# GpSimd's small operations in the order of the text, other places for loads, and a product of seven for the first key projection

## The chip, the cores and the metric

The kernel runs on one core of a Trainium2 chip. The metric is the device time of one execution in microseconds (us). One profiled execution gives the trace; its engines are called PE (TensorE: matmuls), DVE (VectorE), ACT (ScalarE), POOL (GpSimd) and SP (which only issues transfers). ACT and POOL issue transfers too. "PEclk" is the share of full speed that TensorE's clock was granted.

## The reference

Four images of 512 channels and 32x32 positions go through four layers. Each layer normalizes its input over groups of 16 channels and adds its result to the input.

```python
x = x + _L0_conv_ref(_gn(x), ...)   # attention, heads mixed, softmax, attention normalized
x = x + _L1_conv_ref(_gn(x), ...)   # a gate for each channel
x = x + _L2_conv_ref(_gn(x), ...)   # plain attention
x = x + _L3_conv_ref(_gn(x), mempool, 8)  # top 8 of 2048 memory rows
```

- Layer 0 projects queries, keys and values (512x512 weights), forms the scores of 8 heads over 1024x1024 positions, mixes the heads by an 8x8 matrix, takes the softmax, normalizes every head's map by its mean and variance, multiplies by the values and projects.
- Layer 1 takes the mean of every channel, runs 512 amplitudes through a small simulated circuit of 9 qubits (rotations and sign products), and turns 9 results by one more matrix and a sigmoid into a factor for each channel.
- Layer 2 is attention with 8 heads without mixing. Layer 3 looks up memory rows.

All data are 32-bit floats.

## The kernel before

**Stages.** The program first loads image 0, normalizes it, makes its queries (`first`), makes constants (`circuit`) and image 0's keys (`take_k`, line 457). Then layer 0 runs for image 0 to 3 (265 to 290 us each), with the gate of layer 1 of the image before tucked in. Layers 2 and 3 follow. From layer 2 on a flag, `by_scalar`, is set.

**A step of layer 0** (`step`) handles 32 query positions of all heads; an image has 32 steps and 7 more that drain the pipeline ("the tail"). In step s, PE forms scores in two halves (line 510), ACT copies each to the tile `ss` (line 516), and eight transfers, the relays, rearrange the two halves into `s2` (shown as `s<-ss`, line 525): four issued by SP, four by POOL. `ss` has two buffers. Two steps later PE mixes heads (line 536), ACT takes exponentials (line 543), and DVE transposes (549) and gathers statistics (564). From step 7 on PE multiplies by the values (575). Sums of rows (`sums`), their inverses and the scaling of outputs on POOL (`scale`, line 648) go on every four steps.

**Work of other images inside the steps.** `state["plan"]` is a table from step to loads, called by `early` between the two halves of the scores. It holds `next_image` (the next image's rows into `xn_all` in 256 KB halves, and four column blocks of its query weights), and for images 1 to 3 `collect` (the attention output of the image before back into `xn_all`, and its projection weights). These loads are issued by ACT (`beside`). From step OUT = 12 on, `put_quarter` projects a quarter of a block of the previous image's output in each step, in the bank `pt`, and adds it on DVE (727) to `xr`, a piece of the input that `image_piece` loads at the end of the odd step before.

**Chains in moves.** `mid` advances several generators by one move in each step: the normalization of the next image (`prepare`, at steps 9 to 12 and later), the normalization of the attention maps (`instance_norm`, steps 3 to 6), and `state["behind"]`, the gate of the image before (`gating`). A chain alternates tiny matmuls in `pt` (lines 152, 162, 929, 934, 944, 959), copies by DVE, and tiny POOL operations (157 to 159, 126, 909, 922 to 926, 939, 955 and others).

**What sets the order.** Each engine runs its instructions in one order. An instruction wrapped in `pin` keeps the place that it has in the text; the others are placed by a scheduler that works with priorities and estimated times. Nearly all of PE, DVE and ACT in layer 0 is pinned; of POOL the relays and `sums` are, the chains' small operations are not.

**Products of seven.** `seven` multiplies 2x2 blocks with seven products instead of eight, from sums of blocks that DVE makes (`sums_k`, `add7` and `sub7`, all recorded as line 1041). It serves the key projection of images 1 to 3 (`seven_keys`, matmuls in line 1112) and most projections of layer 2, at the border between two images. There `behind` moves once after each product, as the gate does in `seven_keys`.

Of the kernel before, what the change touches and what calls it, by code (L numbers as in the profile page):

```python
# [41 lines left out]
def fast_net(ctx: ExitStack, tc: tile.TileContext, a: dict, out: bass.AP, flag: bass.AP):  # L42
# [88 lines left out]

    def take_small(dst, ps):

        if by_scalar:
            nc.scalar.copy(dst, ps)
        else:
            pin(nc.vector.tensor_copy(dst, ps))


    def group_coeffs_parts(mean, var, tag):  # L140
# [4 lines left out]
        hold = pin if n == 1 else lambda ins: ins  # L145
# [11 lines left out]
        hold(nc.gpsimd.tensor_sub(dm, mean, gm))  # L157
        hold(nc.gpsimd.tensor_mul(sq, dm, dm))
        hold(nc.gpsimd.tensor_add(sq, sq, var))
# [11 lines left out]
        hold(rsqrt(rstd, ve))  # L171
# [98 lines left out]
    def next_image(b, key, src):  # L270
# [8 lines left out]
        halves = [half(k, n) for k in range(KC) for n in range(T // NB)]  # L279
        plan = {NEXT - 8 + 2 * i: halves[i:i + 1] for i in range(4)}  # L280
# [142 lines left out]
    def prepare(b):  # L423
# [5 lines left out]
        nc.gpsimd.tensor_mul(ybar, dm, rstd)  # L429
        nb = small.tile([P, KC], F32, tag="nb", name=f"nb{b}")  # L430
        nc.gpsimd.tensor_mul(nb, gm, rstd)
        nc.gpsimd.tensor_scalar_mul(nb, nb, -1.0)
# [222 lines left out]
    def collect(b):  # L655
# [10 lines left out]
        def w(m):  # L666
# [4 lines left out]
            OUT - 2: [part(1, 1)], OUT - 1: [w(0)], OUT: [w(1)], OUT + 1: [part(2, 0)],  # L671
            OUT + 2: [w(2)], OUT + 3: [part(2, 1)], OUT + 4: [w(3)], OUT + 5: [part(3, 0)],
            OUT + 6: [part(3, 1)],
# [9 lines left out]
    def instance_norm(b):  # L683
# [7 lines left out]
        nc.gpsimd.tensor_scalar(by_head, of_head, red, None, ALU.mult)  # L691
# [7 lines left out]
        nc.gpsimd.tensor_scalar_add(al, al, IN_EPS)  # L699
        rsqrt(al, al)  # L700
        nc.gpsimd.tensor_mul(al, al, gamma)
        bb = small.tile([P, NH], F32, tag="ibb", name=f"ibb_{b}")
        nc.gpsimd.tensor_scalar_mul(bb, al, -1.0 / T)
        nc.gpsimd.tensor_add(bb, bb, beta)
        nc.gpsimd.tensor_mul(bb, bb, I["vsum"])
# [49 lines left out]
    def put_quarter(b, i):  # L755
# [3 lines left out]
        m, n4 = unit(i)[0], 2 * unit(i)[1] + i % 2  # L759
        Q = NB // 2  # L760
        ps = small_ps(f"p_{b}_{i}")[:, 0:Q]
        o = out_view(b)
        for k in range(KC):
            pin(nc.tensor.matmul(  # L764
                ps, I["w_p"][:, k, m * P:(m + 1) * P], o[:, n4, k],
                start=(k == 0), stop=(k == KC - 1),
            ))
        add_to(b, m, I["xr", m, n4 // 2][:, n4 % 2 * Q:(n4 % 2 + 1) * Q], ps)
        if n4 % 2:
            piece_done(b, m, n4 // 2)  # L770
# [44 lines left out]
    def circuit():  # L815
# [11 lines left out]
        pin(nc.vector.tensor_scalar_mul(m, m, SCALE))  # L827
        pin(nc.vector.tensor_mul(
# [25 lines left out]
        nc.scalar.activation(sincos, ang, AF.Sin)  # L854
# [1803 lines left out]
```

## Time and profile before

| | before |
| --- | --- |
| device time, median of 3 runs | 2538.16 us (2535.89 to 2540.12) |
| the profiled execution's own time | 2539.05 us |
| its span | 2537.3 us |
| PE busy | 2482.0 us, 98% |
| DVE busy | 1803.6 us, 71% |
| POOL busy | 1217.8 us, 48% |
| ACT busy | 1019.2 us, 40% |
| granted PE clock, mean | 0.996 |
| moved by transfers | 367.19 MB, 145 GB/s |

A row of the timeline has the start, the duration, the engine, the line and the operation with what it writes and reads; "x4" counts merged instructions, and the bracket is the idle time of the engine just before, with what ended it. A matmul of 128x512 in 32-bit floats shows as two records. An engine with "q" behind its name is its queue of transfers. In a list of waits the last three numbers are the total, how many times, and the longest. The rows of windows give for every engine the busy time and, in brackets, its instructions, then PEclk, the mean busy share of the 16 transfer engines, and what they moved per second.

### The profile page before, as it was taken

To read this page: it belongs to the slowest core of one execution; us is meant where nothing else is said; L and a number is where in the kernel's file an instruction comes from. 1 tells how busy PE (TensorE), PEld (TensorE's weight loads), DVE (VectorE), ACT (ScalarE), POOL (GpSimd) and SP (SyncE) were. 2 spreads that over 40 slices of the span, in tenths; PEclk is the share of its full clock that TensorE was granted. 3 is DMA by queue.
4 is the path that set the end of the run, shared out by engine and by line. 5 is a ranking of instruction groups with operands and counts; after the bars stand their busy time and mean duration, and the time that the engine had idled before them with its cause. 6 is when DMAs were issued, how large, how long until landed. Compare 5 with 4: busy or idle time off the path is not lost.

```text
span 2537.3 us, 48070 instructions
## 1 busy us (share of the span) xinstructions
PE 2482.0 (98%) x18520; PEld 1177.2 (46%) x18520; DVE 1803.6 (71%) x2940; ACT 1019.2 (40%) x1237; POOL 1217.8 (48%) x1688
## 2 busy tenths in 40 slices
PE   9999999999999999999999999999999999999998
PEld 4344534554355534545633633453363344444445
DVE  4599568875688548885768777576857648787876
ACT  1467346651665336651254145225314612121211
POOL 2266425553355525553185147117405616666665
PEclk9999999999999999999999999999999999999999
DMA  2578548872698528893211330131114046767666
GB/s 84 146 205 236 132 126 222 240 219 73 175 238 235 145 73 210 241 246 136 76 47 54 116 128 18 63 104 51 44 44 150 18 141 180 222 182 222 181 189 176
DMA packets 190031, 367.19 MB, mean 145 GB/s; under 512 B 32985, under 2 KB 96473, under 8 KB 185570
## 3 DMA queue, kind: packets, MB, share of 16 engines
q1 hardware_dynamic: 109712, 186.58, 23.7%
q0 software_dynamic: 49152, 142.79, 20.6%
q10 hardware_dynamic: 30930, 34.66, 5.1%
q8 instruction: 149, 2.44, 0.4%
q14 instruction: 88, 0.72, 0.1%
HBM read 190.10 MB, written 39.58 MB: 91 GB/s over the span
## 4 chain that ended last, share of the span: by engine, by line
PE 65%; issue 10%; POOL 10%; DVE 7%; DMA 5%; ACT 2%; SPq 0%; POOLq 0%; ACTq 0%; DVEq 0%
PE pair L1112 11%; PE pair L1358 7%; PE pv L575 7%; PE pair L199 7%; POOL got L1535 7%; PE pair L510 6%; PE pair L536 5%; PE pt L468 5%; PE pair L1238 4%; PE pt L1395 4%; PE pt L764 3%; PE pv L1395 3%; DMA s<-ss 2%; ACT e L543 2%; DVE eT L1377 1%
## 5 line engine op out<-in xcount | busy, mean ns | idle before, releaser
L549 DVE STREAM_TRANSPOSE eT<-e 128x1024 f32<-128x1024 f32 x256 | 316.6, 1237 | 203.3 <-ACT e L543 202.7
L525 POOL DMA_DIRECT2D s<-ss x512 | 258.0, 511 | 393.9 <-PE pair L536 128.5
L1535 POOL DMA_INDIRECT got<-in_mem,ix x256 | 279.7, 1093 | 214.2 <-DVE tmx L1541 142.0
L1352 ACT ACTIVATE eT<-pair 128x1024 f32<-128x1024 f32 x256 | 248.2, 1022 | 319.9 <-PE pair L1358 158.0
L564 DVE BATCH_NORM_STATS2 st<-e 128x6 f32<-128x256 f32 x1024 | 350.7, 404 | 0.0
L1376 POOL TENSOR_TENSOR e<-eT 128x1024 f32<-128x1024 f32 x96 | 240.4, 2507 | 166.8 <-ACT eT L1352 122.3
L543 ACT ACTIVATE e<-pair 128x1024 f32<-128x1024 f32 x256 | 250.5, 1022 | 164.3 <-PE pair L536 134.2
L516 ACT COPY ss<-pair 128x1024 f32<-128x1024 f32 x256 | 247.3, 1019 | 86.1 <-DMA s<-ss 44.0
L510 PE MATMUL pair<-k,q 64*32 64x512 f32 x4096 | 268.1, 600 | 12.8 <-ACT e L543 12.8
L575 PE MATMUL pv<-eT,v 128*64 128x128 f32 x4096 | 250.7, 276 | 4.0 <-ACT pv L635 4.0
L575 PEld LDWEIGHTS pv<-eT,v 128*64 128x64 f32 x4096 | 221.1, 137 | 71.7 <-issue 55.2
L1358 PE MATMUL pair<-q,k 64*128 64x512 f32 x1024 | 240.0, 605 | 2.0 <-DVE sum L1041 0.9
L1377 DVE TENSOR_TENSOR eT<-eT,e 128x1024 f32<-128x1024 f32 x96 | 142.5, 1485 | 129.4 <-POOL e L1376 129.2
L1372 POOL TENSOR_TENSOR eT<-eT 128x1024 f32<-128x1024 f32 x32 | 83.4, 2606 | 201.3 <-ACT eT L1352 197.4
L536 PE MATMUL pair<-s,wmix 32*32 32x512 f32 x4096 | 160.9, 602 | 6.9 <-DMA s<-ss 5.4
L1582 DVE SCALAR_TENSOR_TENSOR acc<-got,et,acc 128x512 f32<-128x512 f32 x210 | 157.9, 752 | 7.5
L1358 PEld LDWEIGHTS pair<-q,k 64*128 64x128 f32 x1024 | 92.2, 186 | 140.4 <-issue 66.4
L1515 ACT COPY att<-pair 128x1024 f32<-128x1024 f32 (+1 forms) x65 | 64.9, 999 | 221.2 <-PE pair L1510 212.4
L510 PEld LDWEIGHTS pair<-k,q 64*32 64x32 f32 x4096 | 57.2, 105 | 181.0 <-ACT e L543 86.9
L1041 DVE TENSOR_TENSOR k<-k,pair 128x512 f32<-128x512 f32 (+1 forms) x80 | 67.9, 893 | 78.3 <-PE pair L1112 62.1
L1530 DVE MAX8 top<-att 128x8 f32<-128x2048 f32 x31 | 71.1, 2293 | 73.0 <-issue 40.8
L1510 PE MATMUL pair<-memT,xn_d 128*128 128x512 f32 x256 | 120.7, 594 | 0.0
(380 smaller groups left out, 3737.5 us busy)
## 6 DMA issues: line engine op xcount, KB each, us to landing
s<-ss SPq DMA_DIRECT2D x512, 128.0 KB
s<-ss POOLq DMA_DIRECT2D x512, 128.0 KB
rb<-r POOLq DMA_DIRECT2D x64, 128.0 KB
o<-o SPq DMA_DIRECT2D x32, 256.0 KB
xr_c<-x SPq DMA_DIRECT2D x32, 256.0 KB
rb_c<-r SPq DMA_DIRECT2D x64, 128.0 KB
eT<-x SPq DMA_DIRECT2D x32, 256.0 KB
out<-eT SPq DMA_DIRECT2D x32, 256.0 KB
```

The costliest lines, as they stand in the source:

```text
L510: pin(nc.tensor.matmul(sc[m * NS:(m + 1) * NS, r, :], q[r * HD:(r + 1) * HD, m, s * NS:(s + 1) * NS], k_[r * HD:(r + 1) * HD, m, n * NB:(n ...
L516: pin(nc.scalar.copy(ss[:, :, n * NB:(n + 1) * NB], sc))
L525: pin(relays[side].dma_start(out=s2[2 * m + r::NH], in_=ss[m * NS:(m + 1) * NS, r, :]))
L536: pin(nc.tensor.matmul(mixed(s, r // 2)[t * NS:(t + 1) * NS, r % 2, :].rearrange("p (qq k) -> p qq k", qq=2), wmix[r * NS:(r + 1) * NS], s ...
L543: pin(nc.scalar.activation(e[:, half].rearrange("p r qq k -> p (r qq k)"), flat2(mixed(s, half)), AF.Exp))
L549: pin(nc.vector.transpose(eT[:, j % 2].rearrange("p b (qq i r) x -> p i r qq b x", qq=2, i=4)[:, i, 2 * half:2 * half + 2], e[:, half].rea ...
L564: pin(nc.vector.bn_stats(st[:, i, 2 * half + r, qq, :], e[:, half, r, qq, :]))
L575: pin(nc.tensor.matmul(pv[r * HD:(r + 1) * HD, gp, :], I["v"][:, t, g * HD:(g + 1) * HD], eT[:, j % 2, t, :, 4 * g:4 * g + 4], start=(t == ...
L1112: pin(nc.tensor.matmul(ps[:, m, :], w[:, k, m * P:(m + 1) * P], x[:, k, :], start=(k == 0), stop=(k == 1)))
L1352: pin(nc.scalar.activation(e, scs[len(es)], AF.Exp, scale=SCALE))
L1358: pin(nc.tensor.matmul(sc[:, r, :], I["k"][r * HD:(r + 1) * HD, m, t * P:(t + 1) * P], I["q"][r * HD:(r + 1) * HD, m, n * NB:(n + 1) * NB] ...
L1535: pin(nc.gpsimd.indirect_dma_start(out=got[:, i, :], out_offset=None, in_=a["mem"], in_offset=bass.IndirectOffsetOnAxis(ap=ix[:, i:i + 1], ...
```

## The change

- `kept` pins POOL's small operations of the chains as long as `by_scalar` is not set, so in the whole of layer 0; before only calls with one column were pinned.
- For image 1 alone, `next_image` puts its eight half rows and four weight columns one to a step at steps 8 to 19 (before: steps 20 to 33). `collect` swaps some outputs and weight columns between steps 12 and 18.
- `image_piece` is issued in the even step, by `early`, behind the step's other loads. `put_half` writes alternate halves of the bank.
- The first keys come from `seven_keys(0)`; `circuit` becomes a generator whose rotations go between the products.
- In `seven` a function `between` is called after the matmuls of each product and ahead of their evacuation. The gate moves there (`go_on`), leaves the last three steps of the tail, and has one move more before its second rotation. In image 3's tail it goes on into `seven_v`.
- At layer 2's border `behind` moves after products 3, 4, 6 and 7 of the first seven, not after each. The sums of Wq for image 1 start two units earlier.

```diff
     by_scalar = []
 
+    def kept(ins):
+        return ins if by_scalar else pin(ins)
+
...
         n = mean.shape[1]
-        hold = pin if n == 1 else lambda ins: ins
...
         dm, sq = tile_("dm"), tile_("gsq")
-        hold(nc.gpsimd.tensor_sub(dm, mean, gm))
-        hold(nc.gpsimd.tensor_mul(sq, dm, dm))
-        hold(nc.gpsimd.tensor_add(sq, sq, var))
+        kept(nc.gpsimd.tensor_sub(dm, mean, gm))
+        kept(nc.gpsimd.tensor_mul(sq, dm, dm))
+        kept(nc.gpsimd.tensor_add(sq, sq, var))
...
         yield
         rstd = tile_("grstd")
-        hold(rsqrt(rstd, ve))
+        kept(rsqrt(rstd, ve))
...
         halves = [half(k, n) for k in range(KC) for n in range(T // NB)]
+        if b == 1:
+            columns = [load_columns(b, key, a[key], m) for m in range(KC)]
+            return {TC + i: [load] for i, load in enumerate(halves + columns)}
         plan = {NEXT - 8 + 2 * i: halves[i:i + 1] for i in range(4)}
         plan |= {NEXT + i: halves[4 + 2 * i:6 + 2 * i] for i in range(2)}
         plan |= {NEXT + 2 + m: [load_columns(b, key, a[key], m)] for m in range(KC)}
...
-        nc.gpsimd.tensor_mul(ybar, dm, rstd)
+        kept(nc.gpsimd.tensor_mul(ybar, dm, rstd))
         nb = small.tile([P, KC], F32, tag="nb", name=f"nb{b}")
-        nc.gpsimd.tensor_mul(nb, gm, rstd)
-        nc.gpsimd.tensor_scalar_mul(nb, nb, -1.0)
+        kept(nc.gpsimd.tensor_mul(nb, gm, rstd))
...
             OUT - 5: [part(0, 0)], OUT - 4: [part(0, 1)], OUT - 3: [part(1, 0)],
-            OUT - 2: [part(1, 1)], OUT - 1: [w(0)], OUT: [w(1)], OUT + 1: [part(2, 0)],
-            OUT + 2: [w(2)], OUT + 3: [part(2, 1)], OUT + 4: [w(3)], OUT + 5: [part(3, 0)],
-            OUT + 6: [part(3, 1)],
+            OUT - 2: [part(1, 1)], OUT - 1: [w(0)], OUT: [part(2, 0)], OUT + 1: [w(1)],
+            OUT + 2: [part(2, 1)], OUT + 3: [w(2)], OUT + 4: [part(3, 0)],
+            OUT + 5: [w(3), part(3, 1)],
...
-        nc.gpsimd.tensor_scalar(by_head, of_head, red, None, ALU.mult)
+        kept(nc.gpsimd.tensor_scalar(by_head, of_head, red, None, ALU.mult))
...
-        nc.gpsimd.tensor_scalar_add(al, al, IN_EPS)
-        rsqrt(al, al)
-        nc.gpsimd.tensor_mul(al, al, gamma)
+        kept(nc.gpsimd.tensor_scalar_add(al, al, IN_EPS))
+        kept(rsqrt(al, al))
+        kept(nc.gpsimd.tensor_mul(al, al, gamma))
...
-    def put_quarter(b, i):
...
+    def put_half(b, i):
...
+        (m, n), half = unit(i), i % 2
...
-        ps = small_ps(f"p_{b}_{i}")[:, 0:Q]
+        ps = small_ps(f"p_{b}_{i}")
...
         for k in range(KC):
             pin(nc.tensor.matmul(
-                ps, I["w_p"][:, k, m * P:(m + 1) * P], o[:, n4, k],
-                start=(k == 0), stop=(k == KC - 1),
+                ps[:, half * Q:(half + 1) * Q], I["w_p"][:, k, m * P:(m + 1) * P],
+                o[:, 2 * n + half, k], start=(k == 0), stop=(k == KC - 1),
             ))
-        add_to(b, m, I["xr", m, n4 // 2][:, n4 % 2 * Q:(n4 % 2 + 1) * Q], ps)
-        if n4 % 2:
-            piece_done(b, m, n4 // 2)
+        add_to(b, m, I["xr", m, n][:, half * Q:(half + 1) * Q], ps[:, half * Q:(half + 1) * Q])
+        if half:
...
         pin(nc.vector.tensor_scalar_mul(m, m, SCALE))
+        yield
         pin(nc.vector.tensor_mul(
...
         pin(nc.vector.tensor_scalar(ang, ang, lim, -lim, ALU.min, ALU.max))
-        nc.scalar.activation(sincos, ang, AF.Sin)
+        yield
+        pin(nc.scalar.activation(sincos, ang, AF.Sin))
+        yield
...
-        for i in range(NP):
-            for l, m in ((0, turn[:, 0:1]), (1, turn[:, 1:3])):
-                rotate(
...
+        for i in range(NP):
+            for l, m in ((0, turn[:, 0:1]), (1, turn[:, 1:3])):
+                rotate(
...
+                )
+                yield
...
-        nc.gpsimd.tensor_mul(y, dm, rstd)
+        kept(nc.gpsimd.tensor_mul(y, dm, rstd))
...
-                    nc.gpsimd.tensor_scalar_mul(us[:, n], u, a_)
+                    kept(nc.gpsimd.tensor_scalar_mul(us[:, n], u, a_))
...
-                nc.gpsimd.tensor_sub(u_v[:, :, 0], cos_v[:, :, 0], sin_v[:, :, 1])
-                nc.gpsimd.tensor_add(u_v[:, :, 1], cos_v[:, :, 1], sin_v[:, :, 0])
+                kept(nc.gpsimd.tensor_sub(u_v[:, :, 0], cos_v[:, :, 0], sin_v[:, :, 1]))
+                kept(nc.gpsimd.tensor_add(u_v[:, :, 1], cos_v[:, :, 1], sin_v[:, :, 0]))
             return u
 
         u = yield from turned(0, lambda ps: pin(nc.tensor.matmul(
             ps[:, 0:KC], turn[:, 0], y, start=True, stop=True)))
         yield
+        if not by_scalar:
+            yield
...
-        nc.gpsimd.tensor_mul(pr, u, u)
+        kept(nc.gpsimd.tensor_mul(pr, u, u))
...
-        nc.gpsimd.tensor_mul(zr[:, 0:1], zr[:, 0:1], zr[:, 1:2])
+        kept(nc.gpsimd.tensor_mul(zr[:, 0:1], zr[:, 0:1], zr[:, 1:2]))
...
-        nc.gpsimd.tensor_add(gate, gate, fcb)
+        kept(nc.gpsimd.tensor_add(gate, gate, fcb))
...
-        nc.gpsimd.tensor_mul(s1, rstd, gate)
-        nc.gpsimd.tensor_mul(t1, gm, s1)
-        nc.gpsimd.tensor_scalar_mul(t1, t1, -1.0)
-        nc.gpsimd.tensor_scalar_add(s1, s1, 1.0)
+        kept(nc.gpsimd.tensor_mul(s1, rstd, gate))
+        kept(nc.gpsimd.tensor_mul(t1, gm, s1))
+        kept(nc.gpsimd.tensor_scalar_mul(t1, t1, -1.0))
+        kept(nc.gpsimd.tensor_scalar_add(s1, s1, 1.0))
...
-        nc.gpsimd.tensor_mul(sa, s1, rstd)
-        nc.gpsimd.tensor_sub(ta, t1, gm)
-        nc.gpsimd.tensor_mul(ta, ta, rstd)
+        kept(nc.gpsimd.tensor_mul(sa, s1, rstd))
+        kept(nc.gpsimd.tensor_sub(ta, t1, gm))
+        kept(nc.gpsimd.tensor_mul(ta, ta, rstd))
         tb = I["tb"] = small.tile([P, KC], F32, tag="tb", name=f"tb_{b}")
-        nc.gpsimd.tensor_add(tb, t1, bp2)
+        kept(nc.gpsimd.tensor_add(tb, t1, bp2))
...
         for i, (at, uses) in enumerate(SEVEN):
             ps = next_pair()
             multiply(ps, *factors[at])
+            if between:
+                between()
             for *ij, op in uses:
                 if put:
...
-    def seven_keys(b):
...
-    def seven_by_channels(b, name, bias):
...
-                     lambda i, j: dst[:, 2 * i:2 * i + 2, j * NB:(j + 1) * NB], begin)
-
-    def seven_v(b):
+                     lambda i, j: dst[:, 2 * i:2 * i + 2, j * NB:(j + 1) * NB], begin,
+                     between=between)
+
+    def seven_v(b, between=None):
...
     first()
-    circuit()
-    for m in range(KC):
-        take_k(0, m, m + 1)
+    constants = circuit()
+    next(constants)
+    key_sums = sums_k(0)
+    run_some(key_sums, 4)
+    next(constants)
+    for i, _ in enumerate(seven_keys(0)):
+        next(key_sums, None)
+        next(constants)
+    run_out(constants)
...
-        if b > 0 and OUT <= s + 1 < OUT + 16 and s % 2:
-            image_piece(b - 1, *unit(s + 1 - OUT))
         if not putting:
             mid(b, s)
...
+    def go_on():
+        next(state["behind"], None)
+
     def early(b, s):
 
         for load in state["plan"].get(s, ()):
             load()
+        if b > 0 and OUT <= s < OUT + 16 and s % 2 == 0:
+            image_piece(b - 1, *unit(s - OUT))
 
...
         elif b > 0 and OUT <= s < OUT + 16:
-            put_quarter(b - 1, s - OUT)
+            put_half(b - 1, s - OUT)
...
         for s in range(STEPS, STEPS + LAG):
-            step(b, s, lambda b, s: next(state["behind"], None),
+            step(b, s, lambda b, s: go_on() if s < STEPS + KC else None,
                  lambda b, s: qs[s - STEPS](s + 1) if s < STEPS + KC else None)
...
-            for i, _ in enumerate(seven_by_channels(0, "k", bk2)):
-                next(state["behind"], None)
+            for i, _ in enumerate(seven_by_channels(0, "k", bk2, go_on)):
...
-        for m, _ in enumerate(() if last else seven_keys(b + 1)):
-            next(state["behind"], None)
+        for m, _ in enumerate(() if last else seven_keys(b + 1, go_on)):
...
-            for i, _ in enumerate(seven_v(0)):
+            for i, _ in enumerate(seven_v(0, go_on)):
...
-            if s == 9 and b == 0:
+            if s == 7 and b == 0:
                 weights = weight_sums(1, "Wq")
-            if s >= 10 and b == 0:
+            if s >= 8 and b == 0:
                 next(weights, None)
...
-            next(behind, None)
+            if i in (2, 3, 5, 6):
+                next(behind, None)
...
```

## The prediction

> **What bounds the kernel now.** I read the head of the page first, then the list of waits of TensorE, then the timeline around each of its longest waits.
>
> ```profile
> span 2537.3 us, 48070 instructions
> ...
> PE 2482.0 (98%) x18520; PEld 1177.2 (46%) x18520; DVE 1803.6 (71%) x2940; ACT 1019.2 (40%) x1237; POOL 1217.8 (48%) x1688
> ```
>
> TensorE is busy for all but 55 us, so the change can win in two ways: fewer matmuls, or fewer of TensorE's waits. These waits bear on the change (total us, times, longest):
>
> ```profile
> PE pair L536 <- DMA s<-ss: 5.4, 4, 2.4
> PE pt L934 <- POOL amp L926: 5.4, 3, 2.5
> PE pt L152 <- DVE eT L1452: 5.0, 2, 2.6
> ...
> PE pt L944 <- POOL pr L939: 1.9, 2, 1.0
> ...
> PE pt L929 <- DVE ri L602: 1.4, 1, 1.4
> ```
>
> They make 19 us. Some cost more than the list says, since the granted clock falls after them. Windows of 10 us around three of them (the number after the POOL column is the clock):
>
> ```profile
> 256.00:266.00 10.00, 8.30 (x128) 2.98 (x128) 5.72 (x13) 7.29 (x8) 5.64 (x14) 0.83 1.04 235
> 594.00:604.00 10.00, 8.55 (x25) 3.83 (x22) 1.56 (x3) 2.64 (x5) 8.72 (x27) 0.83 0.16 54
> ...
> 1598.00:1608.00 10.00, 7.35 (x20) 3.18 (x19) 6.92 (x9) 3.66 (x7) 0.60 (x3) 1.00 0.32 105
> ```
>
> A clock of 0.83 over 10 us is 3.4 us at half speed, which costs 1.7 us beyond the gap. It follows four gaps: 257 (image 0, step 30), 594 and 884 (gate chains of images 1 and 2), 1177 (image 3). The gap at 1598 has none.
>
> The first row of waits has its cause earlier. Timeline of image 1, steps 11 and 12:
>
> ```profile
> 416.10 1.04 POOL L126 TENSOR_TENSOR grstd_a<-gve_a,mhalf 128x4 f32<-128x4 f32 x1 [4.88 <-DVE gve_a L168]
> ...
> 418.20 2.06 POOL L525 DMA_DIRECT2D s<-ss  x4 [0.31 <-DMA s<-ss]
> ...
> 426.11 1.01 ACT L516 COPY ss<-pair 128x1024 f32<-128x1024 f32 x1 [4.36 <-DMA s<-ss]
> 426.14 0.33 ACTq L268 DMA_DIRECT2D xn_all<-o  x1
> 426.20 2.12 PE L536 MATMUL pair<-s,wmix 32*32 32x512 f32 x32 [0.98 <-DMA s<-ss]
> ```
>
> The rsqrt L126, not pinned, stands ahead of GpSimd's four relays of step 11 and waits 4.88 us for VectorE. The scores were copied by 413.2, yet the relays go out at 418.2. ACT's next copy but one needs that buffer and starts late, and TensorE waits. Counted from the first score matmul of a step to that of the next, steps 12 and 13 of image 1 take 7.62 and 8.81 us, where steps 20 and 21 take 7.11 and 6.77.
>
> Last, a wait of the gate chain and one of the border between two images of the third layer:
>
> ```profile
> 595.74 0.38 PE L934 MATMUL pt<-amp,turn 128*128 128x2 f32 x2 [1.45 <-POOL amp L926]
> ```
>
> ```profile
> 1601.64 0.39 PE L152 MATMUL pt<-mv_d,gavg 128*128 128x4 f32 x2 [2.65 <-DVE eT L1452]
> ```
>
> In both, a tiny matmul is pinned ahead of a large product that is ready.
>
> **What the Trainium skill says.** "TensorE: Matmul & The Clock Gate", What's actually happening: the array drops to half rate after an idle window of about 3.4 us and is judged in windows of that length. The trace has half-rate spells of that length, but after gaps of only 1.45 to 2.49 us, so the measurement decides. "DMA: Bandwidth & Descriptors", Issuing engines are not separate DMA queues: transfers of all queues share 16 engines and interleave. The trace agrees: 444 to 454 shows them busy 0.98 at 258 GB/s with three queues at work. So moved loads do collide with the relays.
>
> **The change, part by part.**
>
> *Key projection of image 0.* L199 takes 0.43 us a record, two records a matmul. 32 matmuls become 7 products of 4: 8 records times 0.43 is 3.44 us saved. What is added is VectorE work: sums (1.22 us for 128x1024, 0.69 for 128x512) and 16 adds of about 0.64. Four of the seven groups of sums run between 24.9 and 31 us, where VectorE waits for w_head until 39.0. Then, with a rotation (0.94 us) after each product from the second, I lay VectorE's work against products of 3.44 us: its last add ends about 67.3, while the first scores need keys at 69.4, because the first value chunk (3.44 us) comes between. Free; without that cover the adds would show by some 2 us. The eight later rotations (8 us) fall where VectorE idles until about 85. Gain 3.4.
>
> *Loads for image 1 at steps 8 to 19.* Eight half rows and four weight columns leave steps 20 to 33. There, steps 29, 30 and 31 take 6.00, 9.34 and 2.39 us; 5.34 is usual for step 29's place, and image 1 takes 5.61 and 1.82 for the others: 5.0 us lost. The new place has its price: steps 8 to 19 (126.2 to 194.5) have a DMA share of 0.78, so 53 us of 68. 12 loads of 0.262 MB at 250 GB/s add 12.6: 66 of 67, nearly full. A relay goes out some 11 us before its mix and lands in about 5, so short queues are covered; I charge 1.5. Gain 3.5.
>
> *GpSimd in the order of the text.* The rsqrt of step 12 then stands behind the relays of step 12. Excess of steps 11 to 13: 1.5 us in image 0, about 2.6, 3.1 and 2.5 in images 1 to 3, with half a microsecond at step 16: 10. Behind it comes the DMA queue: 401.5 to 471.6 is 64.6 us of DMA work in 70.1, so 3 us can go before it is full. I keep 8. Other pinned operations are 0.2 to 0.6 us each, and what they wait for was issued a step earlier.
>
> *Gate chain.* It leaves the last three steps for the seven products, one move after each product's matmuls and ahead of its evacuation, with one move more before L934. Two moves are 6.9 us; GpSimd's eight operations (L922 to L926) take 2 to 3.4. So L934 and L944 find their inputs. Removed: 1.45 + 0.97 + 1.7 of clock in image 1, 1.47 + 0.95 + 1.7 in image 2, 1.43 + 2.49 + 1.7 in image 3: 13.9. Added: L959 moves into step 0 of images 2 and 3, right behind a value chunk in the same bank, and waits for ACT's copy (0.6 and the hand-over): 0.75 twice. Queued behind it are the next scores. Gain 12.4.
>
> *Border of the third layer.* The first small matmul moves from product 1 to product 3, about 6.9 us later; its bank is free at 1601.64 and it would ask at about 1605.7. Gain 2.65 + 2.33. Wq's sums two units earlier may also spare part of the 0.70 us at 1380.89; I take 0.5. Gain 5.5.
>
> *Without effect on the sum.* Image pieces go out at about 1.6 us into the even step instead of before it; their add comes 8.2 us after the step's first score matmul (451.87 against 443.71), and by the packet records the row loads of ACT's queue land 2.3 to 6.6 us after issue, these pieces so far at most 4.0: hidden by the step's own matmuls. If late, VectorE waits. Collected rows and columns swap steps at the same bytes; columns keep one step of lead (about 7 us), and land in 3.3 to 7.5: bounded at 0 to 1 us. The half bank instead of a quarter's fixed place removes no wait that TensorE shows.
>
> Sum: 3.4 + 3.5 + 8 + 12.4 + 5.5 = 32.8. The profiled execution took 2539.05 (span 2537.3 and 1.75 around it); less 32.8 is 2506.2. The median shown, 2538.16, is 0.9 lower: 2505 to 2506. I say **2506**, alone 2499 to 2513: the gross terms without my charges make 38.
>
> **Rivals.**
>
> *DMA takes the streaming gain back* (0.15). The share is already 0.98 to 1.04 in places, and the columns move less per second (235 GB/s at 1.04). Then the loads and the relays' punctuality win nothing, 11.5 us: 2517. Against it: 430 to 451 runs at about 260 GB/s without a gap of TensorE.
>
> *VectorE takes the gaps over* (0.10). Without the stall its backlog of adds ends last in the seven products and at the border; a third of 17.9 us stays: 2518. For it: it has 20 to 22 us of work in 25 in image 3's products. Against: image 0's products run back to back in 24.2 us with the same adds.
>
> *The order doesn't change where it hurts* (0.08): L126 still precedes the relays, and only yields and loads work: 8 us less, 2514.
>
> *Slower* (0.04): the later image pieces. 24 of them have 6.6 us to land. If the full queues make each late by over 1.4 us (landing after 8.0), 24 x 1.4 = 34 us of VectorE waits eat the whole gain; at 9 us each the time would be 2538 - 33 + 24 x 2.4 = 2563. The longest landing of a row load in the trace is 6.6, of one issued right behind another.
>
> **How the numbers follow.** The main case has 0.60; 0.03 is left for what I don't see. The range runs from 2496 (38 us gross and a few more) to 2524 (past the rivals' 2518), and leaves out the slower case and the rest. A measurement of this kernel can tell about 0.2% (5 us) from no change: faster 0.95, same 0.02, slower 0.03.
>
> **What would show it.** Right: 56 records for the first key projection; GpSimd's relays of step 11 issued within 1 us of ACT's copy; steps 12 and 13 near 7.1 and 6.8; no half clock near 257, 594, 884, 1177; no L152 wait of over 0.5 at the border. Wrong: VectorE rows ended by a DMA of xr, DMA shares of 1.0 with TensorE waiting for s<-ss in image 0 steps 12 to 20, or new waits for VectorE in the seven products.

## The result and the profile after

| | before | after |
| --- | --- | --- |
| device time, median, same chip (before: the three runs known already and four more) | 2535.89 us (2533.37 to 2540.12, 7 runs) | 2521.16 us (2515.54 to 2530.52, 7 runs) |
| span of the profiled execution | 2537.3 us | 2519.1 us |
| PE busy | 2482.0 us | 2473.0 us |
| PE's waits for a relay (L536 before, L541 after), the rotation (L934, L943), the border (L152, L154) | 5.4, 5.4, 5.0 us | 2.4, 1.5, none |

The ratio is 0.994 with a 95% interval of 0.9923 to 0.9958: 15 us faster. The forecast was 2506, with a range of 2496 to 2524. The sign and the wide range hold, but the result lies outside the 2499 to 2513 given for the main case: about half of the 32.8 us did not come.

The head of the page after, answering the two lines shown of before:

```profile
span 2519.1 us, 48079 instructions
...
PE 2473.0 (98%) x18512; PEld 1174.6 (47%) x18512; DVE 1823.0 (72%) x2962; ACT 1025.3 (41%) x1245; POOL 1225.0 (49%) x1688
```

PE has 8 matmul records less, as seven products instead of eight need; the span fell by twice PE's saved time. TensorE's list of waits after (total us, times, longest):

```profile
PE pt L604 <- DVE xr L732: 3.8, 4, 1.4
...
PE pair L1439 <- DVE s_c L1425: 2.5, 1, 2.5
PE pair L541 <- DMA s<-ss: 2.4, 3, 1.0
PE pt L1408 <- DVE eT L1465: 2.2, 1, 2.2
...
PE pt L968 <- ACT v L477: 1.5, 2, 0.8
PE pt L943 <- POOL amp L933: 1.5, 1, 1.5
```

The waits that the prediction listed are mostly gone. Three others stand there: two of layer 2 (L1439 and L1408), one for VectorE's add to an image piece (L604). Windows of 10 us after (the clock follows the POOL column):

```profile
256.00:266.00 10.00, 9.46 (x134) 5.07 (x119) 7.76 (x17) 8.26 (x9) 6.86 (x16) 1.00 0.84 222
594.00:604.00 10.00, 10.00 (x27) 4.65 (x27) 8.12 (x13) 2.15 (x4) 3.97 (x9) 1.00 0.34 105
...
1338.00:1348.00 10.00, 7.35 (x22) 2.24 (x24) 7.72 (x11) 2.23 (x3) 4.82 (x2) 0.66 0.32 132
1598.00:1608.00 10.00, 10.00 (x29) 4.44 (x28) 6.35 (x9) 0.35 (x2) 1.82 (x5) 1.00 0.43 145
```

The half clocks of layer 0 are gone. A new one stands at 1338, in layer 2: 0.66 over 10 us is 6.8 us at half speed. (A unit of layer 2 is what a step is in layer 0: an image has 16, of some 7.2 us each.)

Where each part of the span went, by the start of the first score matmul of a step, an image or a unit in the two profiled executions:

| stretch | gained, us |
| --- | --- |
| start to the first scores (key projection) | 3.0 |
| image 0, steps 0 to 20 | -1.9 |
| image 0, step 20 to the end of its scores | 4.4 |
| image 0, tail and seven products | -1.5 |
| images 1 to 3, steps 8 to 14 | 5.2 |
| images 1 to 3, step 14 to the end of the scores | -3.1 |
| tails and seven products of images 1 to 3, and steps 0 to 8 of 2 and 3 (gate) | 11.6 |
| layer 2, image 0, units 12 to 15 | -6.7 |
| the three borders of layer 2 | 6.6 |
| the rest | 0.6 |
| sum | 18.2 |

The order did what it should. The timeline after, image 1, answers the lines of step 11 before:

```profile
414.23 1.01 ACT L521 COPY ss<-pair 128x1024 f32<-128x1024 f32 x1 [0.47 <-issue]
...
416.01 2.02 POOL L530 DMA_DIRECT2D s<-ss  x4 [2.10 <-ACT ss L521]
...
418.10 1.04 POOL L126 TENSOR_TENSOR grstd_a<-gve_a,mhalf 128x4 f32<-128x4 f32 x1
```

The relays leave 0.8 us after ACT's copy, and the rsqrt L126 stands behind them.

### The profile page after: what moved, and what is told of

It is laid out like the page before. It is cut to its first block, busy times and chain, and to the rows that moved or that the text cites. A ratio compares the mean times of both kernels' runs of the same rounds, so it can differ in the third digit from the quotient of the medians.

```text
span 2519.1 us, 48079 instructions
## 1 busy us (share of the span) xinstructions
PE 2473.0 (98%) x18512; PEld 1174.6 (47%) x18512; DVE 1823.0 (72%) x2962; ACT 1025.3 (41%) x1245; POOL 1225.0 (49%) x1688
## 4 chain that ended last, share of the span: by engine, by line
PE 85%; DVE 5%; DMA 4%; ACT 3%; issue 1%; POOL 1%; SPq 0%; ACTq 0%; DVEq 0%; POOLq 0%
PE pair L1523 17%; PE pair L1123 12%; PE pair L1371 8%; PE pv L580 8%; PE pair L201 6%; PE pair L515 6%; PE pair L541 5%; PE pt L473 5%; PE pt L1408 4%; PE pv L1408 4%; PE pair L1249 4%; PE pt L769 3%; DMA s<-ss 2%; ACT e L548 2%; DMA xr<-in_x 1%
## 5 line engine op out<-in xcount | busy, mean ns | idle before, releaser
L1390 DVE TENSOR_TENSOR eT<-eT,e 128x1024 f32<-128x1024 f32 x96 | 142.6, 1486 | 133.0 <-POOL e L1389 132.8
L541 PE MATMUL pair<-s,wmix 32*32 32x512 f32 x4096 | 159.3, 600 | 2.7 <-DMA s<-ss 2.4
L1050 DVE TENSOR_TENSOR k<-k,pair 128x512 f32<-128x512 f32 (+1 forms) x96 | 78.1, 858 | 67.8 <-PE pair L1123 54.1
L1408 PE MATMUL pt<-eT,v 128*64 128x512 f32 x512 | 119.6, 610 | 2.2 <-DVE eT L1465 2.2
```

Source lines behind the costliest of these rows:

```text
L541: pin(nc.tensor.matmul(mixed(s, r // 2)[t * NS:(t + 1) * NS, r % 2, :].rearrange("p (qq k) -> p qq k", qq=2), wmix[r * NS:(r + 1) * NS], s ...
L1408: pin(nc.tensor.matmul(pv[r * HD:(r + 1) * HD, :], I["v"][:, t, h * HD:(h + 1) * HD], e[:, r, :], start=(t == 0), stop=(t == TC - 1),))
```

## The experiments

Single profiled executions differ by 1 us here and there, since other relays happen to be late, by up to 3 us where that is frequent, and by up to 4 us in the last 25 us of the program. So each part is read from its own stretch, where it matters over all 14 profiled executions, and the medians stand beside it. Runs of one kernel scatter over up to 15 us: with 4 to 7 runs a side, a difference of 3 to 5 us between two medians is not clear of noise by itself.

**The sums of Wq.** In the changed kernel:

```diff
-            if s == 7 and b == 0:
+            if s == 9 and b == 0:
                 weights = weight_sums(1, "Wq")
-            if s >= 8 and b == 0:
+            if s >= 10 and b == 0:
```

> The changed kernel, with the sums of Wq for image 1 begun at unit 9 of layer 2 again instead of unit 7. Theory: these sums, two units earlier, put VectorE behind at unit 12, so that TensorE waits 2.48 us for s_c and 2.25 us for eT near 1340 and runs 6.8 us at half clock (3.4 us lost): together some 8 us, of which the kernel before had 1.05. Expected: both waits gone, at most one of about 1 us, no half clock near 1340, 2514.5 us (6.7 less than 2521.2). Rival: VectorE is late there for another reason (the border's chain or the clock alone); then the waits stay and the time is 2521 within 2 us.

Measured: 2516.74 us (2511.81 to 2522.81), ratio to before 0.9931 (0.9911 to 0.9951), 4.4 below the changed kernel (the intervals of the two ratios overlap, so the stretch decides). Units 12 to 15 are shorter by 6.67 us, to the hundredth what had been lost; the first border is longer by 1.10. TensorE's timeline with the sums from unit 9:

```profile
1332.02 0.31 PE L1439 MATMUL pair<-s_c,same 128*64 128x32 f32 x4
1333.39 3.65 PE L1408 MATMUL pt<-eT,v 128*64 128x512 f32 x16 [1.06 <-DVE eT L1465]
```

and of the changed kernel, VectorE, GpSimd and TensorE:

```profile
1319.89 0.68 DVE L1050 TENSOR_TENSOR sums<-Wq 128x512 f32<-128x512 f32 x1
...
1322.44 5.57 POOL L1389 TENSOR_TENSOR e<-eT 128x1024 f32<-128x1024 f32 x2 [2.75 <-DVE eT L1390]
...
1325.72 2.84 DVE L1050 TENSOR_TENSOR Wq<-Wq 128x512 f32<-128x512 f32 x1
...
1328.25 2.52 POOL L1385 TENSOR_TENSOR eT<-eT 128x1024 f32<-128x1024 f32 x1 [0.24 <-ACT eT L1365]
...
1328.49 3.38 DVE L1390 TENSOR_TENSOR eT<-eT,e 128x1024 f32<-128x1024 f32 x1
...
1338.41 0.31 PE L1439 MATMUL pair<-s_c,same 128*64 128x32 f32 x4 [2.48 <-DVE s_c L1425]
...
1340.96 1.12 PE L1408 MATMUL pt<-eT,v 128*64 128x512 f32 x2 [2.25 <-DVE eT L1465]
```

The same kind of add takes 0.68 us at 1319.89 and 2.84 at 1325.72; a product L1390 that takes 1.22 alone takes 3.38. Both start while GpSimd works on a 128x1024 product, and end after it. VectorE comes late, two small things of TensorE wait 4.7 us (with the sums from unit 9, 1.06), and the half clock adds 2.9: the sixteen records of L1408 take 6.58 us instead of 3.65. The theory holds: a step that costs VectorE 0.7 us a unit moved other steps under GpSimd's products.

**One sum left out of the crowd.** With the image piece ahead of the other loads (below) and

```diff
-            if s >= 8 and b == 0:
+            if s >= 8 and s != 9 and b == 0:
```

> The changed kernel, with image pieces ahead of the step's other loads, and the sums of Wq begun at unit 7 but with no sum in unit 9. Theory: the sum in unit 9 (0.68 us) is what pushes VectorE's next normalization by 0.6 us, so that the following add, product and scaling fall under GpSimd's 128x1024 products (0.68 becomes 2.84 us, 1.22 becomes 3.38, 0.2 becomes 2.3) and s_c comes 2.48 us late. Without it both waits near 1340 (4.7 us) and the 6.8 us of half clock go, while the border keeps its gain of 1.1: 2521.2 - 6.7 - 2 = 2512.5. Rival: it is the number of sums done by unit 12 that counts; then a wait of 2 us or more stays near 1340 and the time is 2518.

Measured: 2515.95 us (2514.12 to 2520.69), ratio 0.9907 (0.9894 to 0.9921). Half right. Only 4.26 of the 6.67 us came back: the wait for s_c is gone, but the sum in unit 10 is still stretched, to 2.83, and the scaling of the output comes late:

```profile
1337.47 2.87 PE L1408 MATMUL pt<-eT,v 128*64 128x512 f32 x8 [1.77 <-DVE eT L1465]
```

A half-clock window follows. So it is not the sum of unit 9 alone: which VectorE step falls under a GpSimd product depends on the whole row of steps before it.

**The image pieces.** Two places, each in the changed kernel. At the end of the odd step, as before the change:

```diff
         if tiled and part == 3 and s < STEPS:
             take_out(b, j)
+        if b > 0 and OUT <= s + 1 < OUT + 16 and s % 2:
+            image_piece(b - 1, *unit(s + 1 - OUT))
...
         for load in state["plan"].get(s, ()):
             load()
-        if b > 0 and OUT <= s < OUT + 16 and s % 2 == 0:
-            image_piece(b - 1, *unit(s - OUT))
```

> The changed kernel, with the image pieces issued at the end of the odd step again, ahead of the next step's loads. Theory: in the even step they stand behind the step's collected load in the queue and land 4 to 7 us after issue instead of 2.4; their add then waits 14 times on VectorE (27.9 us), TensorE waits for it 4 times (3.8 us), and GpSimd's relays behind it slip. Expected: no wait of the add for a transfer, the steps with waits (image 2 steps 10, 24, 28; image 3 steps 16, 24) shorter by 0.4 to 1.4 us each, 2516 us (5 less). Rival: VectorE's waits are in time that it has to spare and TensorE's come from a backlog that is there anyway; then the time is 2521 within 2 us though the adds no longer wait.

And in the even step, but ahead of that step's loads:

```diff
+        if b > 0 and OUT <= s < OUT + 16 and s % 2 == 0:
+            image_piece(b - 1, *unit(s - OUT))
         for load in state["plan"].get(s, ()):
             load()
-        if b > 0 and OUT <= s < OUT + 16 and s % 2 == 0:
-            image_piece(b - 1, *unit(s - OUT))
```

> The changed kernel, with the image piece still issued in the even step but ahead of that step's other loads. It tells apart why the piece is late. Theory: it is the place behind the collected load; ahead of it the piece lands in about 2.4 us and its completion is seen by 4.5, before the add asks at about 5 to 6.7 us after the issue: the 14 waits (27.9 us) fall to under 3 us in all, and the time is that of the kernel with pieces in odd steps, 2516 us. Rival: the lost lead of 1.4 to 3 us is what counts; then at least 8 of the waits stay, with 15 us or more in all, and the time is 2519 to 2521.

Measured: 2517.35 us (2512.51 to 2521.09), ratio 0.9919 (0.9901 to 0.9938), and 2517.87 (2514.98 to 2522.05), 0.9929 (0.9909 to 0.9949): 3.8 and 3.3 below the changed kernel, each within the noise of so few runs. The stretches say more: from step 14 to the end of the scores of images 1 to 3, the five executions with the piece ahead of the loads (here and below) are 2.5 to 4.3 us shorter than the profile after, and the five with it behind them from 2.5 shorter to 0.6 longer. The means are 2.8 us apart. VectorE's wait for pieces is 27.9 us in 14 places in the changed kernel, none in odd steps, and 8.2 us in 10 when first in the even step; there TensorE no longer waits for it. The place behind the other load makes most of it, the even step the rest: the signal that a piece has landed comes 3.4 us after its issue in odd steps (median of 24), 5.4 when it goes first in the even step, and 6.6 behind the load. That is more than the expectation had for the piece that goes first, and this part of the theory is wrong. The changed kernel's timeline:

```profile
792.84 0.34 ACTq L270 DMA_DIRECT2D xn_all<-in_x  x1
...
793.21 1.18 ACTq L729 DMA_DIRECT2D xr<-in_x  x1
...
802.57 0.48 DVE L732 SCALAR_TENSOR_TENSOR xr<-pt,bproj,xr 128x256 f32<-128x256 f32 x1 [3.52 <-DMA xr<-in_x]
...
808.46 0.38 PE L604 MATMUL pt<-sums,same 128*128 128x32 f32 x2 [1.34 <-DVE xr L732]
```

The piece stands behind a row load. The last data packet of the two ends at 801.82, 8.6 us after the piece's issue (some 2.7 is usual where it goes in the odd step), the signal comes at 802.45, and the add begins at 802.57. The Trainium skill has such a gap: "DMA: Bandwidth & Descriptors", Anatomy of one DMA, says that most of a transfer's fixed 2.0 us is the receipt after its last byte (for transfers that GpSimd issues; this one is ACT's). Here the 14 waiting adds began 0.6 to 1.4 us after the last data packet. How much of VectorE's waiting reaches TensorE differs between executions: 3.8 us in the profile after, 0.9 to 3.6 in four others with the same pieces.

**The loads for image 1.** In the changed kernel, they go back to steps 20 to 33:

```diff
-        if b == 1:
-            columns = [load_columns(b, key, a[key], m) for m in range(KC)]
-            return {TC + i: [load] for i, load in enumerate(halves + columns)}
```

> The changed kernel, with the loads for image 1 at steps 20 to 33 of image 0 again. Theory: the move to steps 8 to 19 gained 4.6 us at the end of image 0 (the wait near 257 and its half clock) and cost about 2 us in steps 8 to 20, where the relays of step 14 now land late (0.99 us wait at 175). Expected: the wait of over 2 us for the relays at step 30 is back, the wait at 175 is gone, 2524 us (2.5 to 4 more). Rival: the pinned order of GpSimd alone cured step 30; then no wait over 1 us comes back there and the time is 2518 to 2520, below the changed kernel.

The same three lines alone, in the kernel before:

> The kernel before, with nothing changed but image 1's twelve loads at steps 8 to 19 of image 0. The prediction's term: the wait of 2.38 us near 257 and its half clock go (step 28 to the end of the scores shorter by 4.6 to 5 us), steps 8 to 20 get longer by 1.5 to 2: 3 to 3.5 us, 2532.7 against 2536. Rival, from the run in which the loads went back: nothing is gained net, since the wait at step 30 comes and goes with the moment at which relays happen to be late; 2536 within 2, with the loss of steps 8 to 20 the same size as the gain at the end.

Measured: 2521.03 us (2519.02 to 2524.89) without the move, where the changed kernel has 2521.16; and 2540.34 (2533.15 to 2545.01, ratio to before 1.0011, 1.0000 to 1.0022) with the move alone. Both gain nothing. In the first, steps 28 to 31 get 2.23 us longer and steps 14 to 20 2.04 shorter. In the second, 4.56 us are won from step 28 to the end of the scores, 3.29 lost in steps 8 to 28 and 1.43 in the tail: 0.2 lost in all.

But the 4.56 is a comparison with one execution. Without the move the end of image 0 took this long only in the profile before, with the wait of 2.38 us and the half clock. With the loads back in the changed kernel the wait at step 30 is 1.17, between the two expectations:

```profile
252.47 2.12 PE L538 MATMUL pair<-s,wmix 32*32 32x512 f32 x32 [1.17 <-DMA s<-ss]
```

In the two kernels with the order alone and the moves alone (below), whose loads were not moved either, it is 0.5 and 1.2. None of the three has a half clock there, and their stretch is 2.4 to 3.1 us shorter than in the profile before. So the move wins 1.5 to 2.2 us against these three. What it costs is in steps 14 to 20: 1.7 to 5.1 us in all ten executions with the move, at most 0.2 in the four without. The rival was right: the wait comes and goes. Windows over 75 us of steps 8 to 19, before and after (the last two numbers are the DMA share and GB/s):

```profile
120.00:195.00 75.00, 70.82 (x1307) 33.60 (x1306) 68.72 (x147) 51.63 (x56) 47.89 (x101) 1.00 0.77 209
```

```profile
120.00:195.00 75.00, 70.20 (x1266) 33.14 (x1270) 67.64 (x147) 50.15 (x55) 46.72 (x99) 1.00 0.92 242
```

At a share of 0.92 relays come late in these steps:

```profile
174.97 2.12 PE L541 MATMUL pair<-s,wmix 32*32 32x512 f32 x32 [0.99 <-DMA s<-ss]
```

The loss moved from one end of the image to the other.

**Order and moves, one at a time.** In the kernel before, only the pins of GpSimd's small operations:

```diff
+    def kept(ins):
+        return ins if by_scalar else pin(ins)
...
-        hold(rsqrt(rstd, ve))
+        kept(rsqrt(rstd, ve))
```

(and so for every operation in the diff of the change).

> The kernel before, with nothing changed but GpSimd's small operations of the chains pinned in layer 0. Theory: the rsqrt no longer stands ahead of the relays of step 11, so the interval from the start of step 12 to that of step 14 gets shorter by about 1.0, 2.1, 2.6 and 1.3 us in images 0 to 3, as between the two kernels: 7 us, 2529 against 2536. The waits of the gate chain (1.45, 0.97, 1.47, 0.95, 2.49) stay, being a matter of distance and not of order. Rival: the steps got shorter because the collected loads swapped places, not because of the order; then the intervals stay within 0.5 us of the kernel before, and the time is 2536 within 2.

Measured: 2539.32 us (2535.62 to 2545.04), ratio 1.0007 (0.9998 to 1.0017): no gain. Steps 12 and 13 got shorter by 1.01, 2.10 and 2.62 us in images 0 to 2 (in image 3, where a relay was late at 994, they did not), so the theory on the stall is right. Its size is partly chance: in the two other executions with GpSimd's operations unpinned (the loads alone, the moves alone) the same steps of images 1 to 3 took 0.3 to 1.6 us less than in the profile before. The means of the 3 unpinned and the 11 pinned executions are 0.8, 1.7, 1.3 and 0.3 us apart in images 0 to 3, about 4 us instead of 7. And the gate pays. In image 3's tail with the order alone, GpSimd:

```profile
1179.79 3.60 POOL L650 TENSOR_TENSOR o<-pv,rb 64x256 f32<-64x256 f32 x4 [0.70 <-issue]
1183.48 0.57 POOL L924 TENSOR_SCALAR ampt<-amp,sincos 128x4 f32<-128x4 f32 x2
...
1185.65 0.20 POOL L941 TENSOR_TENSOR pr<-amp 128x4 f32<-128x4 f32 x1
```

and TensorE:

```profile
1185.91 0.35 PE L946 MATMUL pt<-pr,signs 128*9 128x1 f32 x8 [3.65 <-POOL pr L941]
```

In text order the rotation stands behind the sums of rows and the scaling of four outputs, 8.7 us from 1174.74 to 1183.39. Unpinned, in the kernel before, it slipped in between the sums and came out ahead of the scaling:

```profile
1185.53 0.20 POOL L939 TENSOR_TENSOR pr<-amp 128x4 f32<-128x4 f32 x1
1185.68 3.58 POOL L648 TENSOR_TENSOR o<-pv,rb 64x256 f32<-64x256 f32 x4
```

The wait before the sign products rises from 0.95 to 2.80 us in image 2 and from none to 3.65 in image 3, and image 3's tail gets 3.75 us longer.

The changed kernel, with the gate's moves as before:

```diff
-        if not by_scalar:
-            yield
...
-            step(b, s, lambda b, s: go_on() if s < STEPS + KC else None,
+            step(b, s, lambda b, s: go_on(),
...
-        for m, _ in enumerate(() if last else seven_keys(b + 1, go_on)):
+        for m, _ in enumerate(() if last else seven_keys(b + 1)):
+            go_on()
```

(and so for image 3's two products).

> The changed kernel, with the gate chain moving as before: after each product's evacuation, in all seven steps of the tail, without the additional move. GpSimd's operations stay pinned. Theory: distance in moves is what cured it. The waits before lines 943 and 953 come back (1.4 and 0.95 us in images 1 and 2, about 2.5 in image 3) with half clocks of 3.4 us behind them, and the two waits of 0.77 us for line 968 in step 0 go: 2521 plus 10 to 12, 2531 to 2533. Rival: with its operations in text order GpSimd is early enough anyway; then the waits stay under 0.5 us and the time is 2518 to 2521.

Measured: 2537.22 us (2531.97 to 2545.5), ratio 0.9995 (0.9982 to 1.0008): all of the change's gain is gone. The tails are longer by 5.84, 8.58 and 5.38 us, steps 0 to 8 shorter by 1.79 twice: 16.2 us. More than the 12 expected, because the moves also pay for the order.

The moves alone, in the kernel before (the same edits the other way):

> The kernel before, with nothing changed but the places of the gate chain's moves (after each product's matmuls, four steps of the tail instead of seven, one move more before the second rotation); GpSimd's operations stay unpinned. With the order alone nothing was gained in time (7 us in steps 12 to 14, lost again in the gate's waits, 2.80 and 3.65 us before the sign products), and with the order but the old moves the gate's stretches were 5.8, 8.6 and 5.4 us longer than in the changed kernel. Theory: the moves win by themselves what the prediction gave them, the waits before lines 934 and 944 and the half clocks at 594, 884 and 1177 go: 12 us, 2525 against 2537. Rival: the moves only repair what the order broke; then they win under 6 us alone, since unpinned operations already came early (0.95 us of wait before the sign products) or come at other times than the moves: 2531 to 2537.

Measured: 2529.97 us (2522.80 to 2534.25), ratio 0.9973 (0.9964 to 0.9983), 5.7 faster. The tails give 11.7 us net, as forecast: the theory holds there. But the first border takes 6.56 back (and the second 1.68, where the wait that was there before now draws a half clock):

```profile
1366.49 0.59 PE L152 MATMUL pt<-mv,gavg 128*128 128x4 f32 x2 [3.84 <-DVE eT L1458]
```

With the new moves the gate of image 2 is done before the border, so image 3's chain asks behind the border's first product, where VectorE is late; 6.8 us of half clock follow. In the kernel before it asked behind the second, at 1384.42, and did not wait.

**The border.** The changed kernel moves after each of the seven products again:

```diff
-            if i in (2, 3, 5, 6):
-                next(behind, None)
+            next(behind, None)
```

> The changed kernel, with the border of layer 2 moving after each of the seven products again. In the kernel before with the gate's moves alone, the chain of image 2 ended sooner, so the first border's first small matmul of image 3's chain came behind product 1 and waited 3.84 us (6.8 us of half clock after it), 6.56 us in all. Theory: the four places hold three borders, not two; without them the changed kernel loses about 6.5 us at the first border and 2.9 and 2.6 at the others: 2533, with three waits of over 2 us. Rival, the prediction's reading: only the second and third border wait (2.65 and 2.33 before), the first stays under 1 us: 2526 to 2527.

Measured: 2529.74 us (2525.48 to 2536.39), ratio 0.9973 (0.9963 to 0.9982), 8.6 slower than the changed kernel. The rival was right about the place: the first border loses 0.62 us, not 6.5. What keeps it short is likely the early sums of Wq, which VectorE has behind it there; no run tried that alone. The second and third lose 4.47 and 4.48, more than the 2.9 and 2.6 that the change had won there, since a half-clock window follows each:

```profile
1590.60 0.39 PE L154 MATMUL pt<-mv_d,gavg 128*128 128x4 f32 x2 [2.50 <-DVE eT L1465]
```

**A better version.** Sums of Wq from unit 9 and pieces in odd steps:

> The changed kernel, with the sums of Wq from unit 9 and the image pieces at the end of the odd step: both undone together. Theory: the two are in different stages and add up: 6.67 less in units 12 to 15, 1.1 more at the border, and up to 3 less in steps 12 to 28 of images 1 to 3: 2513.5 (7 less than 2521). Rival: only the sums of Wq count, and the pieces' waits lie in time that VectorE has to spare: 2515.6.

Measured: 2512.39 us (2509.76 to 2512.93, 5 runs), ratio 0.9905 (0.9889 to 0.9921): 23 us faster than before and 8.8 below the changed kernel, about the two parts added (4.4 and 3.8). This difference is clear of noise. And on it, another number of moves before the second rotation:

```diff
-        if not by_scalar:
+        if b == B - 1:
+            yield
             yield
```

> As the kernel with the sums of Wq from unit 9 and pieces in odd steps, and the move that was added before the second rotation taken out for images 0 to 2 and doubled for image 3. In image 3 GpSimd's scaling (10 us of it in a row) stands ahead of the rotation, and a wait of 1.2 to 1.5 us is left before line 943; in images 1 and 2's step 0 line 968 waits 0.77 us and takes 1 us of matmuls and hand-overs with it (1.79 a step, twice). Theory: both go, and with one move less the rotation's eight operations (2 to 3.4 us) just fit into one product of 3.44 us: 2 x 1.79 + 1.5 = 5 us less than without, 2509. Rival: one move is too short: waits of 1 us or more come before line 943 in images 1 and 2, with half clocks (1.7 us each) if they are over 1.4, and the time is the same or up to 3 us more.

Measured: 2518.86 us (2512.90 to 2521.05), ratio 0.9931 (0.9915 to 0.9947), 6.5 slower. The rival holds in images 1 and 2 (waits of 1.01 and 0.53 us, while steps 0 get 1.78 shorter), and in image 3 the wait before the rotation's matmul rises from 1.07 to 3.53: the later move puts the rotation behind more of GpSimd's scaling. With text order, a later place is not an earlier answer.

## Why the prediction was right or wrong

Inside the range by luck, in part: its upper end was drawn for three rivals that each cost 8 to 12 us, and none of them came in full. What ate the gain were two terms read from a single execution (order, loads), and two places where the change pushed other work and the prediction put a gain or nothing (Wq sums, image pieces).

- **Key projection, 3.4.** Right: 56 records, 3.0 us.
- **GpSimd's order, 8 kept of 10.** The mechanism is right: 1.0, 2.1, 2.6 and 1.3 us less between steps 12 and 14. The size was one execution's; over all executions about 4. (The 2 us taken off for a full DMA queue are not worked out either: 64.6 us of work in 70.1 leave 5.5, more than the 3 to be gained.) What failed besides is "Other pinned operations are 0.2 to 0.6 us each, and what they wait for was issued a step earlier": it priced the operations and not the GpSimd work that the text puts ahead of them. By itself the order brought nothing measurable.
- **Gate chain, 12.4.** Right: 11.6 in the change, 11.7 alone. The 0.75 for L968 in step 0 was too small: each of these steps grew by 1.78 (the wait of 0.77 and about 1 us of matmuls moved in, which the tail no longer does). In image 3 L943 still waits, 1.48: two moves cover the rotation's own 2 to 3.4 us, not the scaling ahead of it.
- **Loads, 3.5.** Wrong: nothing. Both sides were mis-sized. The "5.0 us lost" in steps 29 to 31 was one execution's; against three others the move wins 1.5 to 2.2. The charge of 1.5 for fuller queues was 1.7 to 5.1. The rival "DMA takes the streaming gain back" was right on this half; of the other half, the relays' punctuality, about 4 us stayed.
- **Border, 5.0.** Right as the traces stand, 2.9 and 2.6 at the two. It is worth more, since each such wait draws a half clock or not by chance, and since with the late sums of Wq it also guards the first border against the gate's earlier end (no wait there with the sums from unit 9, 6.56 us lost with the moves alone).
- **Wq sums, +0.5.** Wrong, and the largest miss. The first border did gain 1.1, but units 12 to 15 lost 6.67. The step priced what the sums relieve and not what they push. The Trainium skill would have told: "SBUF — State Buffer", Who interferes with whom, says that the two engines share a pair of ports to the on-chip memory under an exclusive lock, and that a VectorE instruction with two inputs from that memory contends with a GpSimd one that reads it. The trace before had the price too: its product L1377 takes 1.22 us or 3.37.
- **Image pieces, 0.** Wrong in the step "these pieces so far at most 4.0: hidden". Three of the 24 pieces before had their last packet only 4.8 to 5.2 us after issue, and the signal up to 6.0. More important, these stood first; the change puts them behind a row load of the same step, where the signal took 4.5 to 9.4. The 0.6 to 1.4 us from the last packet to the add were left out too. The case "slower" had the mechanism (14 of 24 late, 2.0 us each), but most of VectorE's waiting had slack. It cost about 3 us.

Of the 14.6 us between the forecast gain of 32.8 and the span's 18.2, layer 2's units explain 5.6 (5.5 forecast there, -0.05 seen), loads and order together 5.4 (11.5 forecast, 0.9 in image 0 and 5.2 in steps 8 to 14 of the others), the later steps of images 1 to 3 3.1; the rest is within 1 us. This account compares one execution with one, so the chance in the order and the loads is in it. Not settled is why a single relay is late in one execution and not in another, which moves these stretches by 1 to 3 us. No run separates the swapped collected loads or the half bank.

## What to carry to other kernels

Putting an engine's work in text order fixes a bad overtaking and removes good ones: before pinning a chain, read what stands ahead of each of its steps. Moving a small step into a stage costs what it pushes there, so look which operations of the other engine it will fall under, and price a late transfer by its place in its queue and to the instruction that uses it, not to its last packet. Read the size of a stall from several executions: two of the terms here were one execution's. Parts of such a change lean on each other (the order alone won nothing, the moves alone 6 us, and without the moves the whole change won nothing), so undo one at a time before keeping all.

## What the runs showed of the hardware

**Half clock goes by windows.** In all 14 profiled executions every half-rate spell begins on one grid of 3.413 us counted from the first spell. I summed TensorE's idle time in each window of that grid, from 30 us to 5 us before the end. Of the windows at full rate, all 18 with over 2.0 us idle were followed by a half-rate window, 13 of 44 with 1.36 to 2.0, and none with less (89 had 0.9 to 1.36). A window that is itself at half rate needs less: of 11 with over 0.3 us idle, 9 were followed by another. So a gap's position counts. The same wait at the second border lay in two windows in the kernel before (1.55 and 1.10) and with the loads alone (1.42 and 1.28), and cost no clock; it lay in one with the order alone (2.52) and with the moves alone (2.63), and did. What decides between 1.36 and 2.0 stays open. "TensorE: Matmul & The Clock Gate", What's actually happening, has the window's length and that it runs free, which the traces agree with; its idle of a whole window they do not.

**VectorE and GpSimd take turns.** In the profile after, 46 VectorE operations with both inputs in the on-chip memory began inside one of layer 2's GpSimd 128x1024 products (lines 1385 and 1389), and 44 of them ended after it: a sum of 0.68 us took 2.84, a product of 1.22 up to 3.43, the 128x32 operation L1448 of 0.19 up to 2.10. The other two began 5 ns after GpSimd's start and kept their 1.22, and there GpSimd's product took 3.44 and 3.46 us where 2.35 is usual. Ten adds with one input from TensorE's banks (L1465 and some of L1050) began inside too and kept their 0.69 and 1.17 us. That is the rule of the Trainium skill's page "SBUF — State Buffer", Who interferes with whom. Two inputs are not the only way into it: five normalizations L1027, with one large input and a factor and a summand for each partition, took 2.84 to 2.86 us inside such a product and 0.8 outside. No run separates why.
